# Reordering the first-point copies, the bias additions and the TensorE loop of a group norm and convolution layer

## The chip, the cores and the metric

The kernel runs on one core of one Trainium2 chip. The time is the device time of one execution in microseconds (us); the time before is the median of three runs. A profiled execution also has a span, from its first to its last instruction, which is a little shorter than the device time.

The engines go by the profile's short names: PE is TensorE's matrix products and PEld its weight loads, DVE is VectorE, ACT is ScalarE, POOL is GpSimd, and SP is the engine that issues the transfers.

## What is computed

The input is eight images of 32 channels and 128 x 128 points in float32. Each image is normalized in 16 groups of two channels, convolved with 3 x 3 weights, cropped, given a bias, and added to the input. The reference, cut:

```python
def _L0_conv_ref(x, weight, bias, stride, padding):
    ...                                  # fft_H = fft_W = 256
    fout = jnp.einsum('bihw,oihw->bohw', fx, wf)
    sp = jnp.fft.ifft2(fout, norm='ortho').real
    sh = (fft_H - out_h) // 2            # 64
    sw = (fft_W - out_w) // 2
    out = sp[:, :, sh:sh + out_h, sw:sw + out_w]
    return out + bias[None, :, None, None]

def _gn(v, G=16, eps=1e-5):
    ...
    m = jnp.mean(g, axis=(2, 3, 4), keepdims=True)
    s = jnp.var(g, axis=(2, 3, 4), keepdims=True)
    return ((g - m) / jnp.sqrt(s + eps)).reshape(v.shape)

x = x + _L0_conv_ref(_gn(x), L0_conv_weight, L0_conv_bias, 1, 1)
```

The crop starts at row and column 64 of a full convolution of 130 x 130 points, whose rest is zero padding. So only the upper left corner of each output image, 66 x 66 points, has a convolution in it. The rest of the output is the input plus the bias.

## The kernel before

An image lies as 128 partitions (four row and column parities by 32 channels) of 64 x 64 points. In that layout the corner is 33 x 33 points a partition, and the convolution is a product with four 128 x 128 weight tiles, shifted by one row or column. The corner's rows go in three chunks of 11, in one PSUM bank each.

Each image takes these steps:

1. GpSimd copies the image's first point of each partition (`pilot`). TensorE multiplies it with an averaging matrix, and ScalarE turns that into `origin`, a value near the group's mean.
2. ScalarE sums the squares of the image less `origin`; VectorE sums the image.
3. TensorE averages both sums over a group (`group`). ScalarE and VectorE make the reciprocal deviation and the shift (`take_std`).
4. ScalarE normalizes the 34 x 33 or 33 x 33 part that the products need (`normalize`).
5. TensorE multiplies, three chunks of four products each (`multiply`). In float32 each product appears as two matmul records.
6. GpSimd adds the bias to the part of the image outside the corner, in two instructions (`add_bias`). VectorE adds products, bias and input in the corner (`add`).
7. The image is stored, the first four as two pairs.

All eight images are loaded at the start and stay in SBUF; the kernel works on them in place. The parts that matter here, with cuts marked by `...`:

```python
def take_first(img, *needs):
    first_ok[img] = put(
        "pool", lambda e: e.tensor_copy(pilots[img % 2], xts[img][:, 0, 0:1]),
        *rows_in(img, 1), *needs, *([pilot_ok[img - 2]] if img > 1 else []), mark=True,
    )

def pilot(img):
    pilot_ok[img] = put(
        "pe", lambda e: e.matmul(ps_w[:, 0:1], avg, pilots[img % 2], start=True, stop=True),
        first_ok[img], avg_ok, *([origin_ok[img - 1]] if img else []), mark=True,
    )
...
def normalize(img):
    ...
    for rows in (slice(0, ROWS + 1), slice(ROWS + 1, N)) if img == 0 else (slice(0, N),):
        normal[img].append(put("act", ... AF.Identity, ... mark=True))

def add_bias(img):
    xt = xts[img]
    low = xt[:, N:H, :].rearrange("p h w -> p (h w)")      # 1984 points
    right = xt[:, 0:N, N:W]                                # 33 x 31 points
    free = [*normal[img], *sums_ok[img], bias_ok] + ([warm_ok] if img == 0 else [])
    biased[img] = [
        put("pool", lambda e: e.tensor_scalar(part, part, bias_sb, None, op0=ALU.add), *free, mark=True)
        for part in (low, right)
    ]
...
take_first(1, w_ok)
group(0)
warm_ok = keep_warm(0, 1, w_ok)
pilot(1)
take_std(0)
normalize(0)
add_bias(0)
pilot_back(1)
sum_squares(1)
sum_up(1)

put.kept = []
for img in range(B):
    more = img + 1 < B
    if img + 2 == B:
        put.emit_loop(NPAIR - 1, {"act": 2 * 5, "dve": 2 * 5, "pool": 2 * 3})
    multiply(img, 0)
    multiply(img, 1)
    if img:
        add(img - 1, 0, NCHUNK)
        ...                                                # stores
    if img + 2 < B:
        take_first(img + 2)
        pilot(img + 2)
    if more:
        group(img + 1)
        take_std(img + 1, (lambda: pilot_back(img + 2)) if img + 2 < B else (lambda: None))
        normalize(img + 1)
        add_bias(img + 1)
    multiply(img, 2)
    if img + 2 < B:
        sum_squares(img + 2)
        sum_up(img + 2)
...                                                        # last adds and stores
```

`put` sends an instruction to an engine, with the semaphore waits that its needs call for; `mark` makes the instruction count up its engine's semaphore. Instructions of one engine run in the order in which the program puts them. TensorE's are collected, and `emit_loop` writes them as a loop of rounds of two images. In the loop a wait is for a register's value, which grows by a fixed step a round: 10 counts of ScalarE, 10 of VectorE and 6 of GpSimd. A wait's start value is the largest that any round needs, with that round's steps taken off. Before, three rounds are a loop, and the last two images are written out.

Of the kernel before, what the change touches and what calls it, by code (L numbers as in the profile page):

```python
# [30 lines left out]
AF = mybir.ActivationFunctionType  # L31
ALU = mybir.AluOpType

P = 128
# [113 lines left out]
def conv_preact_kernel(nc: bass.Bass, x: bass.AP, wb: bass.AP, out: bass.AP):  # L148
    NPAIR, _, _, H, W = x.shape
# [7 lines left out]
    def sbuf(name, *shape):  # L157
        return nc.alloc_sbuf_tensor(name, list(shape), F32).ap()
# [7 lines left out]
    xts = [pairs[img // 2][:, img % 2] for img in range(B)]  # L166


    wb_sb = sbuf("wb_sb", C, 2, 9 * C)
    loaded = {}  # L170

    def load(to, of):
        name = f"load{len(put.sems)}"
        put.semaphore(name)
        return put("sp", lambda sp: sp.dma_start(to, of), adds=name)  # L175

    for img in range(2):
        loaded[img] = []
        for half in range(2):
            rows = slice(half * H // 2, (half + 1) * H // 2)  # L180
            loaded[img].append((rows.stop, load(xts[img][:, rows, :], x[0, :, img, rows, :])))
            if img == 0 and half == 0:
                weights_in = load(wb_sb[:, :, 0 : 6 * C + 1], wb)
    for img in range(2):
        loaded[2 + img] = [(H, load(xts[2 + img], x[1, :, img]))]
    for pair in range(2, NPAIR):
# [2 lines left out]
    def rows_in(img, last):  # L189

        return [token for k, (_, token) in enumerate(loaded[img]) if k == 0 or loaded[img][k - 1][0] < last]
# [6 lines left out]
    eps = sbuf("eps", P, 1)  # L198
    avg = sbuf("avg", P, P)
    warm = sbuf("warm", P, 1)  # L200
    bias_sb = sbuf("bias_sb", P, 1)
    pilots = [sbuf(f"pilot{k}", P, 1) for k in range(2)]
    eps_ok = put("pool", lambda e: e.memset(eps, EPS * FFT * FFT), mark=True)
# [18 lines left out]
    for k in (0, 1, 3):  # L222
        avg_ok = put(
            "pool", lambda e: e.tensor_copy(avg[:, k * C : (k + 1) * C], avg[:, 2 * C : 3 * C]), sums, mark=True
        )
    none_ok = put("pool", lambda e: e.memset(wb_sb[:, 0, 6 * C + 1 :], 0.0), mark=True)

    put("act", lambda e: e.activation(warm, eps, AF.Sqrt), eps_ok)

    gs = [sbuf(f"g{k}", P, N, N) for k in range(2)]  # L230
    sums = [sbuf(f"sums{k}", P, 2, 2) for k in range(2)]
    unused = sbuf("unused", P, H * W)
    origins = [sbuf(f"origin{img}", P, 1) for img in range(B)]
    squares = [sbuf(f"square{img}", P, 1) for img in range(B)]
    variances = [sbuf(f"var{img}", P, 1) for img in range(B)]
    stds = [sbuf(f"std{img}", P, 1) for img in range(B)]
# [7 lines left out]
    def take_first(img, *needs):  # L244

        first_ok[img] = put(
            "pool", lambda e: e.tensor_copy(pilots[img % 2], xts[img][:, 0, 0:1]),  # L247
            *rows_in(img, 1), *needs, *([pilot_ok[img - 2]] if img > 1 else []), mark=True,
        )

    def pilot(img):
# [5 lines that stand above are left out]
    def parts(img):  # L257

        return [slice(0, H // 2), slice(H // 2, H)] if img == 0 else [slice(0, H)]

    def sum_up(img):
        sums_ok.setdefault(img, [])
# [10 lines left out]
    def pilot_back(img):  # L273
        origin_ok[img] = put(
            "act",
            lambda e: e.activation(origins[img], ps_w[:, 0:1], AF.Identity, scale=-float(NUMBERS // 8)),  # L276
            pilot_ok[img], mark=True,
        )
# [23 lines left out]
                *sums_ok[img], avg_ok, *means_read.get(img - 1, ()), mark=k == last,  # L302
            )

    def take_std(img, between=lambda: None):
        square_ok = put(
            "act",
            lambda e: e.activation(squares[img], ps_ms[:, 0:1], AF.Square, bias=origins[img]),  # L308
            group_ok[img], origin_ok[img], mark=True,
        )  # L310
        var_ok = put(
            "dve",
            lambda e: e.tensor_scalar(variances[img], ps_ms[:, 1:2], squares[img], None, op0=ALU.subtract),  # L313
            square_ok, mark=True,
        )
        between()

        std_ok = put(
            "act",
            lambda e: e.activation(stds[img], variances[img], AF.Sqrt, bias=eps, scale=float(FFT * FFT)),  # L320
            var_ok, mark=True,
        )
        rstd_ok = put("dve", lambda e: e.reciprocal(rstds[img][:, 0:1], stds[img]), std_ok, mark=True)  # L323
        shift_ok = put(
            "dve",
            lambda e: e.tensor_scalar(  # L326
                rstds[img][:, 1:2], ps_ms[:, 0:1], rstds[img][:, 0:1], -1.0, op0=ALU.mult, op1=ALU.mult
            ),
            rstd_ok, mark=True,
        )  # L330
        means_read[img] = (shift_ok,)

    def normalize(img):
        xt, g, rstd = xts[img], gs[img % 2], rstds[img]
        normal[img] = []
        for rows in (slice(0, ROWS + 1), slice(ROWS + 1, N)) if img == 0 else (slice(0, N),):
            normal[img].append(
                put(
                    "act",
                    lambda e: e.activation(  # L340
                        g[:, rows, :], xt[:, LO + rows.start : LO + rows.stop, LO:W], AF.Identity,
                        bias=rstd[:, 1:2], scale=rstd[:, 0:1],
                    ),
                    *means_read[img], *rows_in(img, H), *conv_ok.get(img - 2, ()), mark=True,
                )
            )

    def add_bias(img):

        xt = xts[img]  # L350
        low = xt[:, N:H, :].rearrange("p h w -> p (h w)")
        right = xt[:, 0:N, N:W]
        free = [*normal[img], *sums_ok[img], bias_ok] + ([warm_ok] if img == 0 else [])
        biased[img] = [
            put("pool", lambda e: e.tensor_scalar(part, part, bias_sb, None, op0=ALU.add), *free, mark=True)  # L355
            for part in (low, right)
        ]

    def multiply(img, n):
        g = gs[img % 2]  # L360

        ps = pss[img % 2][:, n, 0 : ROWS * N].rearrange("p (r w) -> p r w", w=N)
        for k in range(4):
            dr, dc = k // 2, k % 2

            rows = min(ROWS, N - dr - n * ROWS)
            top = n * ROWS + dr
            needs = [normal[img][min(n, len(normal[img]) - 1)]] + added.get(img - 2, [])
            ok = put(
                "pe",  # L370
                lambda e, k=k, dc=dc, rows=rows, top=top: e.matmul(  # L371
                    ps[:, 0:rows, 0 : N - dc], w_sb[:, k * P : (k + 1) * P],
                    g[:, top : top + rows, dc:N],
                    start=(k == 0), stop=(k == 3),
                ),
                *needs, mark=k == 3,
            )
        conv_ok[img] = [ok]
# [36 lines left out]

    taps = wb_sb.rearrange("p t k -> p (t k)")[:, 0 : 15 * C].rearrange("p (a b o) -> p a b o", a=5, b=3)
    w5 = w_sb.rearrange("p (dr dc r k) -> p dr dc r k", dr=2, dc=2, r=2)
    places = {  # L420

# [4 lines left out]
    for q in range(4):  # L426
        rin, cin = q // 2, q % 2
        to = slice(q * C, (q + 1) * C)
        bias_ok = put("pool", lambda e: e.tensor_copy(bias_sb[to, :], wb_sb[:, 1, 6 * C : 6 * C + 1]), weights_in, mark=True)
        for dc, c, b in places[cin]:  # L430
            w_ok = put(
                "pool",
                lambda e: e.tensor_copy(  # L433
                    w5[to, :, dc, :, c.start * C : c.stop * C],
                    taps[:, 1 - rin : 5 - rin, b, :].rearrange("p (dr r) b o -> p dr r (b o)", dr=2),
                ),
                w_zero, none_ok, weights_in, mark=True,
            )
    take_first(1, w_ok)
    group(0)  # L440
# [1 line left out]
    pilot(1)  # L442
    take_std(0)
    normalize(0)
    add_bias(0)
    pilot_back(1)
    sum_squares(1)
    sum_up(1)


    put.kept = []
    for img in range(B):
        more = img + 1 < B
        if img + 2 == B:
            put.emit_loop(NPAIR - 1, {"act": 2 * 5, "dve": 2 * 5, "pool": 2 * 3})
        multiply(img, 0)
        multiply(img, 1)
        if img:
            add(img - 1, 0, NCHUNK)
            if img == 2 or img == 4:  # L460
                store(out[img // 2 - 1], pairs[img // 2 - 1], *finished(img - 2, img - 1))
            elif img > 4:
                store(out[(img - 1) // 2, :, (img - 1) % 2], xts[img - 1], *finished(img - 1))
        if img + 2 < B:
            take_first(img + 2)
            pilot(img + 2)
        if more:
            group(img + 1)
            take_std(img + 1, (lambda: pilot_back(img + 2)) if img + 2 < B else (lambda: None))
            normalize(img + 1)  # L470
            add_bias(img + 1)
        multiply(img, 2)
        if img + 2 < B:
            sum_squares(img + 2)
            sum_up(img + 2)
    xt, to = xts[B - 1], out[NPAIR - 1, :, 1]
    store(to[:, N:H, :], xt[:, N:H, :], biased[B - 1][0])
    add(B - 1, 0, 2)
    add(B - 1, 2, NCHUNK)
    stored = store(to[:, 0:N, :], xt[:, 0:N, :], biased[B - 1][1], *added[B - 1])  # L480


    seen = {**put.seen["sp"]}
# [42 lines left out]
```

## Time and profile before

| what | value |
|---|---|
| device time, median of 3 | 111.87 us (110.8 to 112.34) |
| profiled run, device time | 111.99 us |
| its span | 110.0 us |
| mean granted TensorE clock | 0.921 |
| GpSimd waiting for ScalarE's normalize | 21.9 us, 7 times |
| PE weight load of the pilot waiting for GpSimd's copy | 25.5 us, 7 times |
| DMA | 33.61 MB, mean 305 GB/s over the span |

A busy share is an average over the span. The rows by line, engine and operation give how many instructions of a kind there are, the mean duration of one in ns, and what the engine waited for ahead of them. The chain is followed back from the last instruction: at each step to whatever released it, or to the instruction before it on its engine. A step's share of the chain is therefore time on the path that set the end. The clock line has a digit for each fortieth of the span: the tenths of full clock that TensorE was granted.

### The profile page before, as it was taken

The page shows a single profiled execution, that of the slowest core. Times are in us where ns is not written, and L with a number is a line of the kernel's source. Part 1 is how long each engine was busy: PE and PEld are TensorE (multiplying, and loading weights), DVE is VectorE, ACT ScalarE, POOL GpSimd, SP SyncE. Part 2 cuts the span into 40 slices and gives each one's busy share as a digit, 9 for nine tenths or more (in the row PEclk, how much of TensorE's full clock was granted, in tenths as well). Part 3 has the DMA queues.
Part 4 walks back from the last instruction along what each step waited for, and adds up shares of the span by engine and source line. Part 5 has one row for each costly group of instructions (what it writes and reads, how often), then busy time and mean ns, then how long its engine had stood idle before and what let it go on. Part 6 is the DMA issues. An engine that isn't in the chain of part 4 may idle for free.

```text
span 110.0 us, 695 instructions
## 1 busy us (share of the span) xinstructions
PE 75.6 (69%) x232; PEld 45.4 (41%) x232; DVE 50.1 (45%) x42; ACT 47.4 (43%) x53; POOL 72.6 (66%) x51
## 2 busy tenths in 40 slices
PE   0024957967893499919980999568943999989800
PEld 0013434535460356515640666245613566556400
DVE  0085369102990089206950498019910893240130
ACT  5057259602980189006930496029901791510000
POOL 6384007992499519980999069933996199889910
PEclk9999996699999959999999769999999579999985
DMA  3999999999999990498800000898469104969986
GB/s 71 378 354 411 456 420 441 417 476 405 500 417 405 441 488 36 191 572 381 381 0 0 0 0 0 381 572 381 191 286 423 54 0 191 381 286 465 384 332 252
DMA packets 2241, 33.61 MB, mean 305 GB/s; under 512 B 256, under 2 KB 320, under 8 KB 448
## 3 DMA queue, kind: packets, MB, share of 16 engines
q1 hardware_dynamic: 2240, 33.60, 72.8%
q14 instruction: 1, 0.01, 0.0%
HBM read 16.83 MB, written 16.78 MB: 305 GB/s over the span
## 4 chain that ended last, share of the span: by engine, by line
POOL 45%; PE 22%; ACT 12%; DMA 7%; DVE 5%; issue 2%; SPq 1%; POOLq 0%
POOL x L355 44%; PE ps L371 15%; ACT g L340 9%; DMA x<-x_dram 7%; PE ps_w L404 3%; PE ps_w L253 2%; PE ps_m L301 2%; ACT std L320 2%; ACT square L308 2%; DVE rstd L326 1%; DVE var L313 1%; DVE x L386 1%; DVE rstd L323 1%; SPq L175 1%; POOL pilot L247 1%
## 5 line engine op out<-in xcount | busy, mean ns | idle before, releaser
L355 POOL TENSOR_SCALAR x<-x,bias_sb 128x1984 f32<-128x1984 f32 (+1 forms) x16 | 65.0, 4069 | 26.8 <-ACT g L340 21.9
L371 PE MATMUL ps<-g,w_sb 128*128 128x363 f32 (+1 forms) x192 | 66.6, 505 | 3.2 <-ACT origin L276 1.9
L371 PEld LDWEIGHTS ps<-g,w_sb 128*128 128x128 f32 x192 | 39.0, 208 | 26.8 <-issue 6.6
L268 DVE TENSOR_REDUCE sums<-x 128x1 f32<-128x4096 f32 (+1 forms) x9 | 35.4, 3937 | 7.3 <-DMA x<-x_dram 7.3
L287 ACT ACTIVATE unused<-x,origin 128x4096 f32<-128x4096 f32 (+1 forms) x9 | 29.9, 3321 | 0.8 <-DMA x<-x_dram 0.7
L313 DVE TENSOR_SCALAR var<-ps_m,square 128x1 f32<-128x1 f32 x8 | 1.8, 219 | 37.6 <-ACT square L308 37.6
L253 PE MATMUL ps_w<-pilot,avg 128*128 128x1 f32 x16 | 3.2, 267 | 22.1 <-POOL pilot L247 22.1
L308 ACT ACTIVATE square<-ps_m,origin 128x1 f32<-128x1 f32 x8 | 2.1, 261 | 37.5 <-PE ps_m L301 37.5
L386 DVE SCALAR_TENSOR_TENSOR x<-ps,bias_sb,x 128x1089 f32<-128x1089 f32 (+2 forms) x9 | 10.9, 1220 | 7.5 <-PE ps L371 7.5
L253 PEld LDWEIGHTS ps_w<-pilot,avg 128*128 128x128 f32 x16 | 2.7, 204 | 26.0 <-POOL pilot L247 25.5
L340 ACT ACTIVATE g<-x,rstd 128x1089 f32<-128x1089 f32 (+2 forms) x9 | 10.7, 1202 | 3.9 <-DVE rstd L326 3.9
L404 PE MATMUL ps_w<-x,avg 128*128 128x512 f32 x6 | 4.9, 953 | 3.1 <-DMA x<-x_dram 3.1
L247 POOL COPY pilot<-x 128x1 f32<-128x1 f32 x8 | 1.5, 184 | 4.4 <-DMA x<-x_dram 4.4
L301 PEld LDWEIGHTS ps_m<-sums,avg 128*128 128x128 f32 x18 | 3.3, 224 | 1.2 <-issue 1.0
L404 PEld LDWEIGHTS ps_w<-x,avg 128*128 128x128 f32 x6 | 1.6, 302 | 4.2 <-ACT unused L287 3.2
L301 PE MATMUL ps_m<-sums,avg 128*128 128x2 f32 x18 | 3.3, 261 | 0.0
L320 ACT ACTIVATE std<-var,eps 128x1 f32<-128x1 f32 x8 | 2.4, 294 | 1.9 <-DVE var L313 1.9
L276 ACT ACTIVATE origin<-ps_w 128x1 f32<-128x1 f32 x8 | 1.3, 162 | 4.3 <-PE ps_w L253 4.3
L323 DVE RECIPROCAL rstd<-std 128x1 f32<-128x1 f32 x8 | 1.3, 164 | 2.9 <-ACT std L320 2.9
L433 POOL COPY w_sb<-wb_sb 32x128 f32<-32x128 f32 (+1 forms) x8 | 2.5, 339 | 0.0
L326 DVE TENSOR_SCALAR rstd<-ps_m,rstd 128x1 f32<-128x1 f32 x8 | 1.8, 219 | 0.3
L287 ACT ACTIVATION_READ_ACCUMULATOR unused<-x,origin 128x1 f32 x9 | 1.7, 187 | 0.0
(15 smaller groups left out, 6.1 us busy)
## 6 DMA issues: line engine op xcount, KB each, us to landing
x<-x_dram SPq DMA_DIRECT2D x2, 4096.0 KB, 34.1
out_dram<-x SPq DMA_DIRECT2D x2, 4096.0 KB, 11.1
out_dram<-x SPq DMA_DIRECT2D x3, 2048.0 KB, 6.3
x<-x_dram SPq DMA_DIRECT2D x4, 1024.0 KB, 8.5
x<-x_dram SPq DMA_DIRECT2D x2, 2048.0 KB, 18.1
out_dram<-x SPq DMA_DIRECT2D x1, 1056.0 KB, 4.3
out_dram<-x SPq DMA_DIRECT2D x1, 992.0 KB, 4.4
wb_sb<-wb_dram SPq DMA_DIRECT2D x1, 48.2 KB, 4.7
```

What stands on the lines that cost most here:

```text
L253: "pe", lambda e: e.matmul(ps_w[:, 0:1], avg, pilots[img % 2], start=True, stop=True),
L268: lambda e: e.tensor_reduce(sums[img % 2][:, k, 0:1], piece, mybir.AxisListType.X, ALU.add),
L287: lambda e: e.activation(unused[:, rows.start * W : rows.stop * W], piece, AF.Square, bias=origins[img], accum_out=sums[img % 2][:, k, 1:2],),
L301: lambda e, k=k: e.matmul(ps_ms[:, 0:2], avg, sums[img % 2][:, k, :], start=(k == 0), stop=(k == last)),
L308: lambda e: e.activation(squares[img], ps_ms[:, 0:1], AF.Square, bias=origins[img]),
L313: lambda e: e.tensor_scalar(variances[img], ps_ms[:, 1:2], squares[img], None, op0=ALU.subtract),
L320: lambda e: e.activation(stds[img], variances[img], AF.Sqrt, bias=eps, scale=float(FFT * FFT)),
L340: lambda e: e.activation(g[:, rows, :], xt[:, LO + rows.start : LO + rows.stop, LO:W], AF.Identity, bias=rstd[:, 1:2], scale=rstd[:, 0:1],),
L355: put("pool", lambda e: e.tensor_scalar(part, part, bias_sb, None, op0=ALU.add), *free, mark=True)
L371: lambda e, k=k, dc=dc, rows=rows, top=top: e.matmul(ps[:, 0:rows, 0 : N - dc], w_sb[:, k * P : (k + 1) * P], g[:, top : top + rows, dc:N] ...
L386: lambda e: e.scalar_tensor_tensor(part, in0=ps, scalar=bias_sb, in1=part, op0=ALU.add, op1=ALU.add),
L404: "pe", lambda e: e.matmul(ps_w, avg, piece, start=True, stop=True),
```

## The change

It has four parts.

- **First points one image ahead.** The copy of an image's first point goes ahead of the bias additions of the image two before it, where it came after them. The origin is made at the end of the normalization of the image before. It is meant to free TensorE's statistics product from waiting for GpSimd.
- **Four rounds on TensorE.** All eight images are in the loop. For that the rounds must be alike: the second half of image 0's normalization no longer counts, and there are pilots for two images that do not exist (of `eps`) and a statistics product of unused sums.
- **Weights in one piece.** Weights, a zero block and the bias come as 496 values in a row for each of 32 partitions, where they were two pieces of 193. The memset of the part between falls away.
- **Bias additions as multiply by one and add.** The same GpSimd instruction gets two operations in place of one; the values are the same.

The diff, cut to its core:

```diff
-    wb_sb = sbuf("wb_sb", C, 2, 9 * C)
+    wb_sb = sbuf("wb_sb", *wb.shape)
...
-                weights_in = load(wb_sb[:, :, 0 : 6 * C + 1], wb)
+                weights_in = load(wb_sb, wb)
...
-    none_ok = put("pool", lambda e: e.memset(wb_sb[:, 0, 6 * C + 1 :], 0.0), mark=True)
...
-            "pool", lambda e: e.tensor_copy(pilots[img % 2], xts[img][:, 0, 0:1]),
-            *rows_in(img, 1), *needs, *([pilot_ok[img - 2]] if img > 1 else []), mark=True,
+            "pool", lambda e: e.tensor_copy(pilots[img % 2], xts[img][:, 0, 0:1] if img < B else eps),
+            *(rows_in(img, 1) if img < B else ()), *needs, *([pilot_ok[img - 2]] if img > 1 else []), mark=True,
...
+    def sum_nothing(img):
+        sums_ok[img] = [
+            put("act", lambda e: e.activation(warm, eps, AF.Identity), mark=True),
+            put("dve", lambda e: e.tensor_copy(idle, eps), eps_ok, mark=True),
+        ]
...
-                    *means_read[img], *rows_in(img, H), *conv_ok.get(img - 2, ()), mark=True,
+                *means_read[img], *rows_in(img, H), *conv_ok.get(img - 2, ()), mark=rows.start == 0,
...
+        pilot_back(img + 1)
+        normal[img].append(origin_ok[img + 1])
...
-            put("pool", lambda e: e.tensor_scalar(part, part, bias_sb, None, op0=ALU.add), *free, mark=True)
+            put("pool", lambda e: e.tensor_scalar(part, part, 1.0, bias_sb, op0=ALU.mult, op1=ALU.add), *free, mark=True)
...
-            needs = [normal[img][min(n, len(normal[img]) - 1)]] + added.get(img - 2, [])
+            needs = [normal[img][min(n, 1)]] + added.get(img - 2, [])
...
     normalize(0)
+    take_first(2)
     add_bias(0)
-    pilot_back(1)
...
-        if img + 2 == B:
-            put.emit_loop(NPAIR - 1, {"act": 2 * 5, "dve": 2 * 5, "pool": 2 * 3})
         multiply(img, 0)
         multiply(img, 1)
...
-        if img + 2 < B:
-            take_first(img + 2)
-            pilot(img + 2)
-        if more:
-            group(img + 1)
-            take_std(img + 1, (lambda: pilot_back(img + 2)) if img + 2 < B else (lambda: None))
+        pilot(img + 2)
+        group(img + 1)
+        if img + 1 < B:
+            take_std(img + 1)
             normalize(img + 1)
+            take_first(img + 3)
             add_bias(img + 1)
         multiply(img, 2)
         if img + 2 < B:
             sum_squares(img + 2)
             sum_up(img + 2)
+        elif img + 2 == B:
+            sum_nothing(B)
...
+    put.emit_loop(NPAIR, {"act": 2 * 5, "dve": 2 * 5, "pool": 2 * 3})
```

More of the change, by code (lines that the diff above doesn't have):

```diff
@@ L200, in conv_preact_kernel @@
     warm = sbuf("warm", P, 1)
+    idle = sbuf("idle", P, 1)
     bias_sb = sbuf("bias_sb", P, 1)
@@ L232, in conv_preact_kernel @@
     unused = sbuf("unused", P, H * W)
-    origins = [sbuf(f"origin{img}", P, 1) for img in range(B)]
+    origins = [sbuf(f"origin{img}", P, 1) for img in range(B + 1)]
     squares = [sbuf(f"square{img}", P, 1) for img in range(B)]
@@ L303, in group, with take_std @@
             )
-    def take_std(img, between=lambda: None):
+    def take_std(img):
         square_ok = put(
@@ L315, in take_std @@
         )
-        between()
         std_ok = put(
@@ L336, in normalize @@
         for rows in (slice(0, ROWS + 1), slice(ROWS + 1, N)) if img == 0 else (slice(0, N),):
[L337 to L343, printed above, removed]
-                    *means_read[img], *rows_in(img, H), *conv_ok.get(img - 2, ()), mark=True,
-                )
-            )
+            ok = put(
+                "act",
+                lambda e: e.activation(
+                    g[:, rows, :], xt[:, LO + rows.start : LO + rows.stop, LO:W], AF.Identity,
+                    bias=rstd[:, 1:2], scale=rstd[:, 0:1],
+                ),
+                *means_read[img], *rows_in(img, H), *conv_ok.get(img - 2, ()), mark=rows.start == 0,
+            )
+            if ok:
+                normal[img].append(ok)
+        pilot_back(img + 1)
+        normal[img].append(origin_ok[img + 1])
     def add_bias(img):
@@ L414, in conv_preact_kernel @@
     sum_squares(0)
-    taps = wb_sb.rearrange("p t k -> p (t k)")[:, 0 : 15 * C].rearrange("p (a b o) -> p a b o", a=5, b=3)
+    taps = wb_sb[:, 0 : 15 * C].rearrange("p (a b o) -> p a b o", a=5, b=3)
     w5 = w_sb.rearrange("p (dr dc r k) -> p dr dc r k", dr=2, dc=2, r=2)
@@ L428, in conv_preact_kernel @@
         to = slice(q * C, (q + 1) * C)
-        bias_ok = put("pool", lambda e: e.tensor_copy(bias_sb[to, :], wb_sb[:, 1, 6 * C : 6 * C + 1]), weights_in, mark=True)
+        bias_ok = put("pool", lambda e: e.tensor_copy(bias_sb[to, :], wb_sb[:, 15 * C : 15 * C + 1]), weights_in, mark=True)
         for dc, c, b in places[cin]:
@@ L436, in conv_preact_kernel @@
                 ),
-                w_zero, none_ok, weights_in, mark=True,
+                w_zero, weights_in, mark=True,
             )
@@ L444, in conv_preact_kernel @@
     normalize(0)
+    take_first(2)
     add_bias(0)
-    pilot_back(1)
     sum_squares(1)
     sum_up(1)
-    put.kept = []
     for img in range(B):
         more = img + 1 < B
-        if img + 2 == B:
-            put.emit_loop(NPAIR - 1, {"act": 2 * 5, "dve": 2 * 5, "pool": 2 * 3})
+        put.kept = []
+    for img in range(B):
         multiply(img, 0)
@@ L508 @@
             [
-                weight.transpose(1, 2, 3, 0)[:, [1, 2, 0, 1]].reshape(C, 2, 6 * C),
-                np.stack([np.zeros_like(np.asarray(L0_conv_bias)), np.asarray(L0_conv_bias)], axis=1).reshape(C, 2, 1),
+                np.insert(weight.transpose(1, 2, 3, 0)[:, [1, 2, 0, 1]], 2, 0, axis=1).reshape(C, 15 * C),
+                np.asarray(L0_conv_bias).reshape(C, 1),
+                np.zeros((C, 15), x.dtype),
             ],
-            axis=2,
+            axis=1,
         ),
```

## The prediction, made before the changed kernel ran

> **What bounds the kernel now.** I began with busy shares. No engine is full: PE 69%, GpSimd (POOL) 66%, the others under 46%, DMA 72.8%. When no engine is full, waits set the time, so the chain of work that ended last comes next, by engine:
>
> ```profile
> PE 75.6 (69%) x232; PEld 45.4 (41%) x232; DVE 50.1 (45%) x42; ACT 47.4 (43%) x53; POOL 72.6 (66%) x51
> ...
> POOL 45%; PE 22%; ACT 12%; DMA 7%; DVE 5%; issue 2%; SPq 1%; POOLq 0%
> ```
>
> Nearly half of the chain is GpSimd, yet GpSimd idles a third of the span. The chain in order of time shows why; this is one image's round:
>
> ```profile
> 28.97 8.13 POOL x L355 x2
> 37.10 0.14 POOL pilot L247
> 37.24 0.04 issue
> 37.28 0.38 PE ps_w L253 x2
> 37.66 0.24 PE ps_m L301 x2
> ...
> 39.25 1.32 ACT g L340
> 40.57 0.03 issue
> 40.60 0.02 POOLq L87
> 40.61 0.12 issue
> 40.73 8.12 POOL x L355 x2
> ```
>
> Columns: start, duration, what. The loop is closed: the bias additions of one image (8.13 us); then, on GpSimd, the copy of the first point of a later image; the pilot product with it; and only behind that, because TensorE works in order, the statistics product, which was ready long before. Then square, variance, root, reciprocal, shift and normalize, and the next bias additions. From 28.97 to 40.73 is **11.76 us an image**. The windows cut at those starts give the same length, with POOL busy 8.25 and PE 8.41 to 9.83 in each.
>
> The last round is free of this: no first point is copied for an image that does not exist. The timeline there:
>
> ```profile
> 87.73 8.12 POOL L355 TENSOR_SCALAR x<-x,bias_sb 128x1984 f32<-128x1984 f32 x2 [3.50 <-ACT g L340]
> ...
> 93.64 0.28 PE L301 MATMUL ps_m<-sums,avg 128*128 128x2 f32 x2
> ...
> 96.73 7.35 PE L371 MATMUL ps<-g,w_sb 128*128 128x363 f32 x24 [0.40 <-ACT g L340]
> ```
>
> The statistics product starts at 93.64 while GpSimd still adds bias (87.73 to 95.85), and the round takes 96.73 - 87.6 = 9.1 us, although its start ran at half clock. This is my model of the changed kernel.
>
> Last, the clock:
>
> ```profile
> PEclk9999996699999959999999769999999579999985
> ```
>
> In windows of 1 us it is 0.50 from about 17.7, 38.0, 61.9 and 85.8, each time for some 3.5 us. The last three dips follow PE idle stretches of 3.35 us (33.93 to 37.28, 57.44 to 60.79, 80.94 to 84.29), all waits for the pilot; stretches of 2.2 us (46.79 to 49.04) brought none.
>
> [...] for copies, (392 - 286)/128 = 0.83 ns an element, [...] for this addition: the two forms give (5281 - 2858)/(1984 - 1023) = 2.52 ns an element, three times a copy. [...] VectorE reduces and adds throughout, and the bias additions stay at 5281 ns mean, 5292 at most. [...] The weights go as 64 rows of 772 B; here their issue takes 0.66 us against 0.39 us for the load before it.
>
> ```profile
> L355 POOL TENSOR_SCALAR x<-x,bias_sb 128x1984 f32<-128x1984 f32 x8 | 42.2, 5281 | 26.8 <-ACT g L340 21.9 <-ACT origin L276 4.9
> ...
> L355 POOL TENSOR_SCALAR x<-x,bias_sb 128x1023 f32<-128x1023 f32 x8 | 22.9, 2858 | 0.0
> ```
>
> **The change, part by part.** *First points one image ahead.* The copy for the image after next now stands ahead of the bias additions, not behind them. The pilot no longer waits for those, so nor does the statistics product. In the new round TensorE limits: two chunks of products at full clock, 16 of the 24 in 7.35 us, 7.35 x 16/24 = 4.9 us; pilot 0.25 and statistics 0.24; from its end to the next image's first product 2.7 (26.14 to 28.85) to 2.8 (93.92 to 96.73), with the third chunk (2.55 us) inside that time. Sum: 4.9 + 0.5 + 2.8 = **8.2 us**. The sums are in time: squares take 3.70 + 0.19 us after normalize, the reduction 4.41 us from 1.4 us before its end, both under 4.9. TensorE idles 0.3 us a round, not 3.35, so I expect no dips in the middle.
>
> *Four rounds.* The loop now covers all eight images; waits inside it are a start value plus a step per round. The order of instructions shows the second half of image 0's normalization without a mark, so the counts agree in every round and the first product waits for the first half only. Before, it started at 17.13, 1.9 us idle, on the next origin; the first half ended at 15.45 + 0.72 = 16.17. That wins 0.9 us and probably the first dip, since the idle stretch before it shrinks from 1.9 to about 1 us. Added: one register step per image between chunks 0 and 1, and for images that do not exist two pilots and one statistics product; in the last image some 0.5 us on TensorE before the last chunk.
>
> *Weights in one piece.* Half as many rows, each 1984 B; up to 0.27 us less issuing ahead of image 0's second half. I take 0.2 us.
>
> *Multiply by one and add.* 16 instructions, 65.0 us together. No row tells what the second operation costs. Nobody adds a multiplication by one unless it takes a quicker path, so quicker is likeliest (65 in 100), unchanged 25, slower 10.
>
> *The sum, TensorE's path.* First product at 16.2 - 0.2 = 16.0; plus 4.9 = 20.9; the squares of image 1 end near 20.9 too (17.18 + 3.71, plus 0.19 for the accumulator, less 0.2). Statistics end at 21.4; image 1 starts at 24.2; six rounds of 8.2 put image 7 at 73.4. Before, image 7's first product to the end took 110.0 - 96.73 = 13.3 us; with 0.5 us of added products 13.8. Span **87.2 us**.
>
> *GpSimd's path at the old speed.* The first additions now stand behind the copy of image 2's first point, which waits for its load. The two 2 MB loads take 18.1 us in the median, from issues near 3.5, and follow each other by some 5 us: image 2 lands near 19.2. Additions start at 19.4 and are then dense: 8 x 8.12 + 7 x 0.28 for the copy and issue = 66.9, end 86.3. The last store took 110.0 - 105.6 = 4.4 us: span **90.7 us**. That exceeds 87.2, so GpSimd at the old speed would bound the end by 3.5 us; quicker, it drops out.
>
> The measured time lies 1.9 us over the span (111.99 beside 110.0): 89.1 or 92.6 us.
>
> **Rivals.** *GpSimd is the new bound.* If the two-operation form costs a third more, 10.8 us an image, additions end at 19.4 + 8 x 10.8 + 2 = 108, the span is 112 and the whole gain is gone. For it: two operations instead of one, on an engine already slow here. Against: the form was chosen on purpose. *TensorE's clock still dips.* Each dip costs up to 1.8 us (half of 3.5); three would give 94.5 us. [...] Against: no idle stretch over 1 us should remain. *Transfers bound the end.* 33.6 MB at the 420 to 440 GB/s seen when busy is 78 us; loads run to 42 us, stores need 40 us more. Stores could start near 37, image 6's near 75, and about 4 MB then remain, 9 to 10 us: the end at 85 to 88, just hidden, but a 1 us slip could show. *Register waits.* [...] before, such steps stood only ahead of statistics and between images.
>
> **The range and the chances.** 89.1 with quick additions, plus about 1 us for register steps and transfers, is 90; 92.6 with unchanged ones. Weighted by 65 to 25, and with a little for dips, I say 90.5. Low end: no added cost and a shorter tail, 87. High end: old speed with two dips, 97. Slower by over 2% needs additions more than a third costlier: 0.04. Within 2%: 0.03. Faster: 0.93.
>
> **What would show each step.** The chain without a GpSimd-to-pilot step in each round; image starts 8.2 us apart; the wait of the pilot's weight load for GpSimd's copy, 25.5 us before, near zero; PEclk at 9 throughout the middle; first product near 16.0; bias rows far below 5281 and 2858 ns, with GpSimd waiting for normalize, or else equal to these and GpSimd dense from 19.4 to 86. Wrong would be: rows above 7000 ns; a GpSimd copy stalled behind a load, holding up additions and then pilots; rounds above 9 us at full clock, a wait that I have not seen; or an end with the stores queued behind one another.

## The result, and the profile after

The changed kernel takes **86.85 us** (median of 4, 86.19 to 87.32) where the kernel before took 111.81 us beside it: a ratio of 0.777, interval 0.770 to 0.785. The prediction said 90.5 us, 87.0 to 97.0. The direction and the mechanism held; the time lies 0.15 us under the range, because terms of the sum were too large. Executions over 1.5% above the fastest of their kernel, among them two of four with the form alone and four of the twenty with the old order in three rounds, are left out of ratios, but not of medians and ranges.

From the page of the changed kernel, four lines: busy time of each engine, the clock, the share of 16 DMA engines, and the chain's shares by engine.

```profile
PE 69.0 (81%) x238; PEld 42.8 (50%) x238; DVE 50.1 (59%) x43; ACT 48.0 (56%) x55; POOL 32.3 (38%) x52
...
PEclk9999999999999999999999999999999999999999
...
q1 hardware_dynamic: 2208, 33.62, 93.4%
...
PE 59%; ACT 17%; DMA 8%; DVE 8%; issue 2%; SPq 1%
```

GpSimd's busy time fell from 72.6 to 32.3 us, and GpSimd, 45% of the chain before, is gone from it. The clock has no dip left. Transfers, 72.8% before, fill 93.4% of a shorter span.

The chain in order of time (start, duration, what), from the first product of image 0, with one whole round and the start of image 7:

```profile
15.20 5.08 PE ps L380 x16
...
31.48 5.07 PE ps L380 x16
36.55 0.12 PE ps_w L253 x2
36.66 0.24 PE ps_m L308 x2
...
38.25 1.31 ACT g L346
39.56 0.06 ACT origin L283
39.62 5.07 PE ps L380 x16
...
72.17 5.07 PE ps L380 x16
```

The loop of waits is now two chunks of products, pilot, statistics, the chain of small operations, normalize, next image. No GpSimd step stands between the products and the pilot. A round is 39.62 - 31.48 = 8.14 us, where it was 11.76.

The groups by form and the waits of the changed kernel (a wait: total us, times, longest):

```profile
L364 POOL TENSOR_SCALAR x<-x,bias_sb 128x1984 f32<-128x1984 f32 x8 | 15.4, 1923 | 23.0 <-ACT origin L283 18.0 <-ACT warm L264 5.0
...
L364 POOL TENSOR_SCALAR x<-x,bias_sb 128x1023 f32<-128x1023 f32 x8 | 9.1, 1138 | 0.0
```

```profile
PEld ps_w L253 <- POOL pilot L247: 6.1, 1, 6.1
POOL pilot L247 <- DMA x<-x_dram: 19.0, 6, 7.2
```

The bias additions take 1923 and 1138 ns instead of 5281 and 2858. The pilot's wait for GpSimd fell from 25.5 us in 7 waits to a single one at the start, ahead of image 0's own pilot. GpSimd's copies, now ahead of the additions, wait for the loads of their images instead: 19.0 us in 6 waits, where it was 4.4 us in 2. The prediction named such a stall as a sign of being wrong. It came, and held up additions (those of image 0 start at 18.70, 3.5 us after its first product), but no pilot of TensorE.

### The profile page after: what moved, and what is told of

Read it like the earlier page. It is cut to its first block, busy times and chain, and to the rows that moved or that the text cites. A ratio compares the mean times of both kernels' runs of the same rounds, so it can differ in the third digit from the quotient of the medians.

```text
span 85.6 us, 726 instructions
## 1 busy us (share of the span) xinstructions
PE 69.0 (81%) x238; PEld 42.8 (50%) x238; DVE 50.1 (59%) x43; ACT 48.0 (56%) x55; POOL 32.3 (38%) x52
## 3 DMA queue, kind: packets, MB, share of 16 engines
q1 hardware_dynamic: 2208, 33.62, 93.4%
HBM read 16.84 MB, written 16.78 MB: 393 GB/s over the span
## 4 chain that ended last, share of the span: by engine, by line
PE 59%; ACT 17%; DMA 8%; DVE 8%; issue 2%; SPq 1%
PE ps L380 50%; ACT g L346 12%; DMA x<-x_dram 8%; PE ps_w L413 4%; PE ps_m L308 3%; ACT std L326 3%; ACT square L315 3%; DVE rstd L332 2%; DVE var L320 2%; DVE x L395 2%; DVE rstd L329 2%; PE ps_w L253 1%; SPq L175 1%; ACT origin L283 0%
## 5 line engine op out<-in xcount | busy, mean ns | idle before, releaser
L380 PE MATMUL ps<-g,w_sb 128*128 128x363 f32 (+1 forms) x192 | 61.0, 466 | 2.9 <-ACT origin L283 2.2
L380 PEld LDWEIGHTS ps<-g,w_sb 128*128 128x128 f32 x192 | 35.1, 189 | 24.2 <-ACT origin L283 5.8
L364 POOL TENSOR_SCALAR x<-x,bias_sb 128x1984 f32<-128x1984 f32 (+1 forms) x16 | 24.3, 1530 | 23.0 <-ACT origin L283 18.0
L253 PEld LDWEIGHTS ps_w<-pilot,avg 128*128 128x128 f32 x20 | 3.9, 202 | 8.4 <-POOL pilot L247 6.1
L308 PE MATMUL ps_m<-sums,avg 128*128 128x2 f32 x20 | 3.8, 264 | 0.0
```

The source lines that it names most:

```text
L308: lambda e, k=k: e.matmul(ps_ms[:, 0:2], avg, sums[img % 2][:, k, :], start=(k == 0), stop=(k == last)),
L364: put("pool", lambda e: e.tensor_scalar(part, part, 1.0, bias_sb, op0=ALU.mult, op1=ALU.add), *free, mark=True)
L380: lambda e, k=k, dc=dc, rows=rows, top=top: e.matmul(ps[:, 0:rows, 0 : N - dc], w_sb[:, k * P : (k + 1) * P], g[:, top : top + rows, dc:N] ...
```

## The experiments

My theory: the closed loop of additions, copy, pilot and statistics set the time, and either half of the change, order or form, is enough to break it. The rivals: one of the two did it alone, and the other, or the loop and the weights, gave a part of their own.

### The form alone

The kernel before, with one line changed:

```diff
-e.tensor_scalar(part, part, bias_sb, None, op0=ALU.add)
+e.tensor_scalar(part, part, 1.0, bias_sb, op0=ALU.mult, op1=ALU.add)
```

> The kernel before with the multiply-and-add form alone; order, loop and weights stay as before. Theory A (the parts overlap: each of order and form alone breaks the closed loop of GpSimd and pilot): bias additions take 1923 and 1138 ns, 3.04 us an image, so the first-point copy behind them is ready 3.4 us after normalize, inside the 4.9 us of the first two chunks. The round falls from 11.76 to about 8.2 us, the pilot's wait for the copy (25.5 us) nearly vanishes, the clock stays full in the middle, and the time is about 90 us (first product near 17.1, perhaps one clock dip there, six or seven rounds of 8.2, tail 13.3). Theory B (the order is what mattered, the form is a small help): the time stays above 100 us.

The four executions took 88.73, 89.86, 91.08 and 91.13 us. The ratio is 0.801 (0.793 to 0.809), of 89.3 us, the mean of the first two. The chain of the execution of 91.08 us, from images 0 to 2:

```profile
16.84 6.63 PE ps L371 x16
...
26.53 5.08 PE ps L371 x16
...
34.66 5.08 PE ps L371 x16
```

Rounds are 8.13 us from image 1 on, with the old order. The first product starts at 16.84, 1.6 us after the changed kernel's, and its 16 products took 6.63 us instead of 5.08: the clock was 0.50 for about 3.5 us there, after TensorE had idled for 2.0 us, as it was in the kernel before (6.77 us, after 1.9 us idle). Image 7's products start 3.1 us after the changed kernel's, all of it from this start. The mean clock was 0.956 in the execution of 89.86 us as well, and 0.980 in that of 88.73 us. So one line brings some 22 of the 25 us, and most of the rest lies in the start.

### All but the form

The changed kernel with the single addition back, the same line the other way.

> The changed kernel with the single addition put back. Theory A (GpSimd at the old speed becomes the bound, as the prediction's second path has it): bias additions of 5281 and 2858 ns stand almost gapless from about 18.7 us, 8 x 8.12 + 7 x 0.28 = 67 us, to 85.7; the last store 4.2 us more; span about 90, time about 91 us; the chain goes to GpSimd. Theory B (GpSimd stays off the path, or the first-point copies stall behind it and hold up TensorE): 87 us as with the new form, or rounds well over 8.4 us and a time above 95 us.

It took 89.81 us (89.72 to 90.12, n = 4), ratio 0.805 (0.801 to 0.810), 3.0 us above the changed kernel. The shares of the chain by engine, and its last image but one and last:

```profile
POOL 66%; DMA 18%; issue 9%; SPq 2%; POOLq 0%
```

```profile
68.41 4.12 POOL x L364
72.52 1.12 issue
73.64 2.85 POOL x L364
76.50 0.13 POOL pilot L247
76.63 8.09 POOL x L364 x2
```

GpSimd is dense from 19.02 to 84.72, 8.23 us an image, and sets the end; TensorE keeps its rounds of 8.14 and is done first. Theory A held: the order without the form also breaks the loop, and then the slow additions become the bound. They start late because the copy ahead of them waits for image 2's load, which lands at 18.71; with the old order, further down, they start at 16.41.

### Old order, with the quick and the slow form

The changed kernel with the copies behind the additions again:

```diff
-            take_first(img + 3)
             add_bias(img + 1)
+            take_first(img + 3)
...
-    take_first(2)
     add_bias(0)
+    take_first(2)
```

> The changed kernel with the first-point copies back behind the bias additions, the quick form kept. Theory A (order and form do the same work; once additions take 3.04 us the order is worth nothing): the copy is ready about 3.4 us after normalize, inside the 4.9 us of the first two chunks; rounds stay at 8.14 us and the time at 86.8, within 0.4 us. Theory B (the order has a worth of its own): some wait of the pilot for the copy appears, rounds above 8.3 us, over 1 us more in all.

86.78 us (86.14 to 87.19, n = 6), against 86.80 for the changed kernel. Once the additions take 3.04 us, the new order is worth nothing that these runs can see.

With the single addition besides:

> The changed kernel with both the old order and the single addition; only weights and the four rounds remain of the change. Theory A (the closed loop of additions, copy, pilot and statistics is back): rounds of 11.75 us, the pilot waiting for the copy some 23 to 26 us in all, clock dips after idle stretches of 3.35 us, and a time of about 109 to 111 us, below the kernel before by the earlier start alone. Theory B (the four rounds or the weights carry a part of the gain that the other runs gave to order and form): under 106 us.

**120.09 us** (119.38 to 121.06, n = 4), 1.076 (1.069 to 1.084) of the kernel before. The loop is back: additions start at 16.41, 28.64 and 40.45, rounds of 12.23 and 11.81 us in turn, and the pilots wait 33.9 us. But the expectation, 109 to 111 us, missed the time by 9 us or more. The timeline of the last image shows what I had left out:

```profile
100.28 8.12 POOL L364 TENSOR_SCALAR x<-x,bias_sb 128x1984 f32<-128x1984 f32 x2 [3.55 <-ACT warm L264]
108.36 0.19 POOL L247 COPY pilot<-eps 128x1 f32<-128x1 f32 x1
...
108.59 0.38 PE L253 MATMUL ps_w<-pilot,avg 128*128 128x1 f32 x2 [3.40 <-POOL pilot L247]
...
109.18 4.10 PE L380 MATMUL ps<-g,w_sb 128*128 128x363 f32 x8
```

The pilot of an image that does not exist waits for GpSimd's copy behind 8.12 us of additions, and image 7's last chunk waits behind that pilot. Image 7's statistics wait in the same way for another such pilot. To settle that this is the cause, the same kernel with three rounds, and so without those pilots:

```diff
-        pilot(img + 2)
-        group(img + 1)
+        if img + 2 < B:
+            pilot(img + 2)
```

> Old order and single addition as in the run that took 120.1 us, but with three rounds in the loop, so without pilots and statistics for images that do not exist. Theory A (in the old order those pilots, too, wait behind 8.1 us of additions: image 7's statistics by 2.7 us, its last chunk by 3.4, and the end of the additions no longer lies beside the products): without them the last round is free as in the kernel before, and the time is 109 to 110.5 us, the kernel before less its later start. Theory B (the new place of the origin's making, behind normalize, or the loop itself is what cost 8 us): 117 us or more.

111.58 us (110.33 to 113.08, n = 20), 0.998 (0.995 to 1.000) of the kernel before: 8.5 us come back. This run takes out the fourth round and the padding together, so it is the two waits in the traces that name the padding as the cause. The further 1 us that I expected from the earlier start did not show in the time: additions start at 16.19, not 17.20, but image 7 at 96.14, only 0.6 us before the old 96.73. In the profile the rounds alternate between 12.2 and 11.8 us. The three longer ones are those where the pilot comes at half clock: pilot and statistics take 0.6 and 0.44 us there, not 0.38 and 0.24. In the profile of the kernel before no round is longer than 11.8.

| time in us, weights in one piece | quick form | single addition |
|---|---|---|
| new order, four rounds | 86.80 | 89.81 |
| old order, four rounds | 86.78 | 120.09 |
| old order, three rounds | not run | 111.58 |

### Which forms are quick

Two variants of the changed kernel, each with its one line altered and each run once: the bias added first and the result multiplied by one,

```diff
+e.tensor_scalar(part, part, bias_sb, 1.0, op0=ALU.add, op1=ALU.mult)
```

> One look at the order of the two operations: add the bias, then multiply by one. Theory A (any two operations take the quick path): 1923 and 1138 ns as in the changed kernel. Theory B (only multiply followed by add is quick): the rows stay at 5281 and 2858 ns or rise, and the time is about 91 us or more.

and a single multiplication,

```diff
+e.tensor_scalar(part, part, bias_sb, None, op0=ALU.mult)
```

> One look at a single operation of the other kind: multiply by the bias value, no second operation (this leaves the addition of the bias out and multiplies the part outside the corner instead, so the output differs). Theory A (a single operation is slow, whatever it is): 5281 and 2858 ns. Theory B (the slow one is the addition as such): about 1923 and 1138 ns.

The groups of the first and then of the second (mean ns after the busy time):

```profile
L364 POOL TENSOR_SCALAR x<-x,bias_sb 128x1984 f32<-128x1984 f32 x8 | 15.4, 1920 | 22.2 <-ACT origin L283 17.2 <-ACT warm L264 5.0
```

```profile
L364 POOL TENSOR_SCALAR x<-x,bias_sb 128x1984 f32<-128x1984 f32 x8 | 42.3, 5282 | 0.0
```

86.51 and 89.71 us, one execution each. The smaller instructions take 1132 and 2862 ns. Both orders of two operations are quick, and a single operation is slow, multiplication as well as addition. An element costs (1923 - 1138)/961 = 0.82 ns with two operations and (5282 - 2862)/961 = 2.52 ns with one. GpSimd's copies of 256 and of 128 elements a partition in the kernel before took 392 and 286 ns, (392 - 286)/128 = 0.83 ns an element. Why a single operation is the slow one, no run says.

### Weights in two pieces again

The changed kernel with the old weight array, its load and its memset:

```diff
-    wb_sb = sbuf("wb_sb", *wb.shape)
+    wb_sb = sbuf("wb_sb", C, 2, 9 * C)
...
-                weights_in = load(wb_sb, wb)
+                weights_in = load(wb_sb[:, :, 0 : 6 * C + 1], wb)
```

> The changed kernel with the weights again in two pieces of 193 values for each of 32 partitions, and the memset between them. The first product of the changed kernel began at 15.20 us, where the prediction had 16.0; the second half of image 0 had landed at 8.53 instead of 9.55 us. Theory A (the weights' small packets held up the loads): the half lands near 9.5 us again, every later event moves by about 1 us, and the time is about 87.8 us. Theory B (the earlier landing is the spread between executions): no difference over 0.3 us.

87.53 us (87.29 to 87.69, n = 6) beside 86.80 (86.64 to 87.08, n = 6) for the changed kernel. The two ranges do not touch. The chain's transfer of image 0's second half, of the changed kernel and then of this one:

```profile
1.72 6.81 DMA x<-x_dram
```

```profile
1.96 7.29 DMA x<-x_dram
```

It is issued 0.24 us later and lands at 9.25 instead of 8.53. One piece is worth 0.7 us: a third of that is the shorter issue (0.42 against 0.66 us) and the rest is transfer. The traces of the other kernels agree: the half lands between 8.3 and 8.9 us in all that have one piece, and between 9.2 and 9.7 in the three that have two.

The changed kernel ran beside it and met its expectation:

> The changed kernel once more, unchanged, as the measure for the three kernels that run beside it. All theories: 86.9 us, within 0.5 us.

### Three rounds

```diff
+        if img + 2 == B:
+            put.emit_loop(NPAIR - 1, {"act": 2 * 5, "dve": 2 * 5, "pool": 2 * 3})
...
-    put.emit_loop(NPAIR, {"act": 2 * 5, "dve": 2 * 5, "pool": 2 * 3})
```

with the products for missing images taken out.

> The changed kernel with three rounds in TensorE's loop and the last two images written out, so without the pilots and the statistics product of images that do not exist. Image 0's second half stays without a mark. Theory A (the loop itself costs and gives nothing, the added products cost): the 0.36 us of pilots and statistics fall away from the last image, and 0.12 us from image 6: time about 86.4 us, 0.4 us less. Theory B (the loop pays because instructions written out come late): a wait of TensorE's for issue in the last two images, time 0.5 us or more above the changed kernel's.

87.01 us (86.85 to 87.57, n = 6), where the changed kernel took 86.80 (86.64 to 87.08): the ranges overlap, and neither theory's difference is there. TensorE ended at 78.72 instead of 80.00 (0.7 us of that is an earlier first product, at 14.47), yet the span was 85.6 both times, and the last store took 5.3 us to land instead of 4.0. What TensorE gives up early, the transfers keep.

### How near the transfers are

A quarter of the products left out, to see what stops next:

```diff
-        for k in range(4):
+        for k in range(3):
```

> The changed kernel with three of the four products in each chunk; it leaves a quarter of the convolution's products out, so the output differs. It asks how near the transfers are. Two chunks take 3.7 us instead of 4.9, and a round is then set by the squares (3.9 us after normalize) plus 0.24 and 2.8, about 7.0 us. Theory A (TensorE's round alone sets the end): image 7 starts at 15.2 + 7 x 7.0 = 64, its products end near 70, span about 76, time about 77 us. Theory B (transfers, 80 us of packet time on 16 engines after a start of 1 to 2 us, are the next bound): the span stops at about 82 us, time about 83 us, with the DMA share above 96%.

83.52 us (83.41 to 84.0, n = 4), ratio 0.749 (0.745 to 0.753). Its last products end at 71.9, 8 us before the changed kernel's, but its span is 82.2. The issuing engine's waits, and the windows (length, PE busy and count, clock, DMA share, GB/s):

```profile
SPq L501 <- DMA out_dram<-x: 8.4, 1, 8.4
```

```profile
40.00:60.00 20.00, 17.20 (x62) 1.00 0.99 419
60.00:75.00 15.00, 10.77 (x40) 1.00 0.99 423
75.00:80.00 5.00, 0.00 (x0) 0.65 0.98 415
```

The share is 1.0 from 2 to 40 us as well, so the transfers are full to the end. Theory B: about 82.2 us of span is what these 33.6 MB allow in this order. The two kernels below stop at 82.6 and 82.4 us.

### Normalizing in two pieces, a faster version

Every image's normalization is split as image 0's was:

```diff
-        for rows in (slice(0, ROWS + 1), slice(ROWS + 1, N)) if img == 0 else (slice(0, N),):
+        for rows in (slice(0, ROWS + 1), slice(ROWS + 1, N)):
```

> The changed kernel with every image's normalization in two pieces as image 0's is: 12 rows first (717 ns), 21 rows after (955 ns, no mark). Theory A (TensorE's round is bound by statistics to normalize, 2.8 us beside a third chunk of 2.55): the first product no longer waits 0.31 us in each of 7 rounds, so 2.2 us less, 84.7 us. Theory B (transfers, busy 93.4% of the span, set the end anyway): TensorE ends earlier but the last stores queue, and the time falls by less than 1 us.

**83.67 us** (83.61 to 83.85, n = 6), 0.749 (0.746 to 0.752) of the kernel before and 3.1 us under the changed kernel. The chain:

```profile
50.61 0.22 PE ps_m L308 x2
50.83 7.22 PE ps L380 x24
58.05 0.12 PE ps_w L253 x2
58.17 0.22 PE ps_m L308 x2
58.39 7.22 PE ps L380 x24
```

All small operations have left its rounds; TensorE runs without a gap. A round is 7.56 us, 0.58 less than 8.14. Half of that is the 0.31 us of waiting. The other half I had not counted: 24 products without a pause take 7.22 us, where 16 and 8 with a pause between them took 5.07 and 2.42; no run says why. TensorE ends at 75.93, 4 us earlier, but the span only falls 3.0, to 82.6, at 96.6% DMA share. Both theories had a part: first TensorE's round, then the transfers.

Last, the same kernel with a shorter end:

```diff
     add(B - 1, 0, 2)
+    store(to[:, 0 : 2 * ROWS, :], xt[:, 0 : 2 * ROWS, :], biased[B - 1][1], *added[B - 1])
...
-            *conv_ok[img], bias_ok, mark=True,
+            chunk_ok[img, last - 1], bias_ok, mark=True,
...
-    stored = store(to[:, 0:N, :], xt[:, 0:N, :], biased[B - 1][1], *added[B - 1])
+    stored = store(to[:, 2 * ROWS : N, :], xt[:, 2 * ROWS : N, :], biased[B - 1][1], *added[B - 1])
```

> The kernel with every normalization in two pieces, and its end changed: the last image's first two chunks are added to the input when their own products are done, and their rows are stored apart, so only 11 rows (352 KB, not 1056) are left behind the last product. Theory A (the end is the last product, the last addition, the last store): addition 0.59 instead of 1.48 us and a store 1 to 2 us shorter, 81.5 us. Theory B (transfers are full, 96.6% of the span, so the last store waits its turn whenever it is issued): within 0.5 us of 83.67 us.

83.69 us (83.54 to 83.87, n = 6): no gain. The last addition did shrink from 1.48 to 0.60 us and ends at 76.49, but the end waits 5.5 us for its transfer.

## Why the prediction was right and wrong

**Right: what bounded the kernel, and how the bound breaks.** The closed loop is shown by taking it apart: rounds of 8.1 us with order or form alone, 11.8 to 12.2 with neither. That TensorE keeps the program's order shows in the times of the kernel before: the last sum of an image was done at 32.49 us, and its statistics product started at 37.66, right behind the pilot. The round's sum, 4.9 + 0.5 + 2.8 = 8.2, measured 5.07 + 0.36 + 2.71 = 8.14: that it is so near is in part luck, since two terms err by 0.1 to 0.2 us in opposite directions. TensorE's clock stayed full, as forecast: 0.998 in the mean, with waits of 0.3 us ahead of the products. The length of an idle stretch alone does not settle it, though: in the kernel before, 1.9 us came before a dip to 0.50, and 2.2 us brought none. GpSimd as the bound at its old speed was right in kind: span 88.8, predicted 90.7; the copy and issue between additions cost 0.11 us an image, not 0.28.

**Right by a guess: the form.** That the two-operation form would be quicker rested on the intent of whoever wrote the change; it was given 65 in 100, and no view of the kernel before showed it.

**Wrong: the sizes, all to one side.** From 90.5 to 86.85 is 3.65 us. The terms of the sum:

| term | predicted | measured | difference, us |
|---|---|---|---|
| first product | 16.0 | 15.20 | -0.8 |
| seven rounds, to image 7 | 57.4 | 56.97 | -0.4 |
| image 7 to the end | 13.8 | 13.4 | -0.4 |
| device time over the span | 1.9 | 1.3 | -0.6 |
| register steps and transfers, added on top | 1.0 | none seen | -1.0 |
| weight given to the unchanged form and dips | 0.4 | 0 | -0.4 |

The largest step that failed is "plus about 1 us for register steps and transfers". For the register steps it was my estimate; no trace had shown such a cost. Two chunks take as long in the kernel before, without the added step, as in the changed kernel with it:

```profile
28.85 5.08 PE L371 MATMUL ps<-g,w_sb 128*128 128x363 f32 x16 [0.32 <-ACT g L340]
```

```profile
39.61 5.08 PE L380 MATMUL ps<-g,w_sb 128*128 128x363 f32 x16 [0.32 <-ACT origin L283]
```

Nor did the transfers add to the end: the last store landed after 4.0 us, and 4.3 before.

The next step is "The measured time lies 1.9 us over the span". It came from one execution of the kernel before, and an unusual one. Over 52 other executions of that kernel the difference has a median of 1.45 us; nine of them have 1.9 to 2.4, and the other 43 have 1.3 to 1.5. The changed kernel's profile has 86.87 - 85.6 = 1.3.

Then the weights, sized at 0.2 us from the issue alone; the runs give 0.7, as the transfer, too, is quicker. The other 0.3 us of the early first product lie within the spread between executions: with two pieces the half landed at 9.25 to 9.70 us in three traces.

The last weighing also has a slip: 65 parts of 90 us and 25 of 92.6 give 90.7, so 90.5 has no room for dips in it. The low end, "no added cost and a shorter tail", left no room for an earlier start as well.

**The rivals.** Transfers were named as hidden, "but a 1 us slip could show". They were nearer than that sounds: the changed kernel stands 3.4 us of span above their floor, and with three rounds an earlier end of TensorE brings no shorter span. The four rounds themselves give no time in the quick kernel (86.80 against 87.01), and with old order and slow additions their padding costs 8.5 us. The 0.9 us that I credited to starting on the first half of image 0 came with the missing mark, which the run with three rounds keeps. I did not try it apart. The form alone (89.3 us) and the old order with the quick form (86.78) are 2.5 us apart; the weights are 0.7 of that and the four rounds nothing, so about 1.8 us should be this mark, with the clock's dip at the first products. This is an estimate from those runs, not a measurement.

## What to carry to other kernels

When an engine is far from full and yet heads the chain, look for a small operation of it that another engine's queue must pass, behind a long one that nobody is waiting for; moving the small one ahead or making the long one short break the same loop, and their gains do not add: here the kernels with one of the two took some 22 us less than the kernel before, the changed kernel 25. Padding the loop with work for rounds that do not exist was free here where that work waited for nothing slow (86.80 us against 87.01), and cost 8.5 us where it waited for slow additions. After a gain of a fifth, ask at once what stands next: here transfers left room for 3 us more, which splitting each image's normalization took.

## What the runs showed of the hardware

- GpSimd's tensor-scalar with one operation takes 2.52 ns an element here, addition or multiplication; with two operations, in either order, 0.82 ns, against 0.83 of a copy.
- The step of a register between two chunks of products left no gap that the trace shows: 16 products in 5.08 us with it (changed kernel) and without (kernel before).
- 14 KB more of weights (62.0 and 48.2 KB), in 32 rows of 1984 bytes and not 64 of 772, let the load behind it land 0.7 us earlier (8.53 and 9.25 us).
